# Keys that wait in DRAM with 32 rows per head, and the order of the adds behind a top-1 expert layer

## The chip, the cores and the metric

The kernel runs on one core of one Trainium2 chip, as a single launch. The metric is the time of one execution on the device in microseconds (us). A core has five engines that run side by side, each through its own list of instructions in order: TensorE (PE in the profile, its weight loads PEld), VectorE (DVE), ScalarE (ACT), GpSimd (POOL) and SyncE (SP). They wait for each other by semaphores. SP does not compute; it issues DMA transfers, which 16 DMA engines carry out. ACT and POOL issue some as well.

## The reference, cut to what matters

Eight layers change x, which has 2 batches of 512 tokens with 256 features. Each adds its result, times the tanh of a gate, to x, and starts from a layer norm of x, the last one included. Four of them are attentions to a context of 1024 tokens per batch, and four are feed-forward layers of different kinds.

```python
x = x + tanh(g_xattn[0]) * L0_xattn(ctx, ctx, layernorm(x), ...)   # 5 sampled places per head
x = x + tanh(g_ffn[0])   * L0_ffn(layernorm(x), rhs)               # int8
x = x + tanh(g_xattn[1]) * L1_xattn(layernorm(x), ctx, ctx, ...)   # 16 heads of 8
x = x + tanh(g_ffn[1])   * L1_ffn(layernorm(x), Wg, bg, W1, W2)    # 8 experts, top 1
x = x + tanh(g_xattn[2]) * L2_xattn(layernorm(x), ctx, ctx, ...)   # 16 heads of 16
x = x + tanh(g_ffn[2])   * L2_ffn(layernorm(x), ...)               # ternary weights
x = x + tanh(g_xattn[3]) * L3_xattn(layernorm(x), ctx, ctx, ...)   # 8 heads of 4
x = x + tanh(g_ffn[3])   * L3_ffn(layernorm(x), ...)               # channel mix
```

An attention (l1, l2, l3 below) is, for each head, softmax(scale · Q Kᵀ) V with K and V from the context, and an output product. The expert layer is

```python
gate_scores = softmax(xf @ Wg + bg);  top1 = argmax(gate_scores)
gate = gate_scores * one_hot(top1) / (its sum over tokens + EPS) * T
out  = sum over e of gate[..., e] * (relu(x @ W1[e]) @ W2[e])
```

## The kernel before, in words

x stays in SBUF as 8 blocks of 128 tokens by 256 features: blocks 0 to 3 are batch 0, blocks 4 to 7 batch 1. The context stays there too, transposed.

The kernel is written with a framework that is given tiles (buffers with a tag and a number of copies) and instructions, and that sets semaphores and the order of each engine's instructions by a planner. Where the text calls `keep_in_program_order`, the instruction stays where the program has it. SP keeps at most eight DMAs in flight: each issue first waits for the eighth before it. All its DMAs share one ring on each of the 16 DMA engines, so on one engine they go one after the other; ACT's and POOL's DMAs have rings of their own.

**Keys and values of the attentions.** They depend on the context alone, so they are computed early, in gaps of other layers. During layer 0, `context_1` (L967) computes l1's keys and the values of l1 and l3. TensorE makes `pk` or `pv`, ACT copies it into a staging tile (`kst` L938, `v1st` L983, `v3st` L985, two copies of each tag), and SP stores that to DRAM: K_l1, V_l1, V_l3. In the expert layer `context_2` (L993) computes l2's values, which stay in SBUF, and the keys of l2 and l3, which go to DRAM as K_l2 and K_l3. `prepare_context` (L910) declares these DRAM tensors at the beginning of `context_1`. K has HD + 1 rows of 2048 keys per head (HD is 8, 16 and 4), and the last row, stored from a tile of ones, takes part in the softmax: the query side carries the negated maximum there.

**loaded_keys** (L1013) brings keys to SBUF for groups of four heads. A tile KT has 128 partitions by 2048 keys: head h of the group has partitions 32h to 32h + HD, and the rest of its 32 partitions must be zero, since the score products (L1143, L1174) contract over 32 partitions. So POOL sets the whole tile to zero (L1019), and SP loads each head by a DMA of HD + 1 rows of 8 KB (L1021). l1 and l2 have four groups, l3 has two: 10 memsets and 40 loads. KT tiles have the tag "wide", four buffers that other layers' weights use also.

**Who calls it.** l1's keys and values are loaded at the end of layer 0, when its buffers come free (L1809); the int8 layer runs there. l2's keys are loaded at the end of `moe_ffn` (L1422), each tile when the weights of an expert leave its buffer. l3's are loaded at the end of the ternary layer, from `ternary_ffn` (L1687), before a branch (L1689) that is taken for weights that are not ternary.

**Layer 0** (`window_attention`). For each batch, DVE and ACT make the weights of the sampled places (`window_weights`, L596 to L631, with an exp on ACT at L618). TensorE transposes them (`tpA`), ACT copies that to AT (L440), TensorE spreads AT over the features (L467), and DVE multiplies with the values (`pv` L482, eight per batch).

**The expert layer.** Rows of x are scattered to the experts' places in a DRAM tensor xg, each expert's rows are loaded, go through its two products, and the result `ye` is stored by ACT to the DRAM tensor yg (L1408), two stores per expert. `rest` (L1424) then gathers, per batch, four blocks of rows by an indirect DMA on POOL (L1427) and adds them to x on DVE, times the gate (L1434).

**attention** (L1038) takes `rest` as `before`. It first runs it for batch 0; then batch 0's norm and queries (`queries(0)`) alternate, piece by piece, with `rest` for batch 1. The norm (`statistics` L149, `normalized` L173) is, per batch: statistics of four blocks (L156, L157), variance + eps on DVE (L160), square root on ACT (L161), reciprocal on DVE (L162), the shift nb (L168), h on ACT (L184); TensorE transposes h (L1070) and multiplies by the query weights (L1076).

Of the kernel before, what the change touches and what calls it, by code (L numbers as in the profile page):

```python
# [20 lines left out]
F32 = mybir.dt.float32  # L21
# [4 lines left out]
ALU = mybir.AluOpType  # L26
AX = mybir.AxisListType

P = 128
B, S, D = 2, 512, 256  # L30
M = 1024
# [43 lines left out]
def _bc(ap, shape):  # L75

    return ap.broadcast_to(shape)


class _Net:  # L80
# [829 lines left out]
    def prepare_context(self):  # L910
        nc = self.nc
        self.kd, self.vd = {}, {}
        for name, H, HD in (("l1", 16, 8), ("l2", 16, 16), ("l3", 8, 4)):
            k = self.dram.tile([H, HD + 1, B * M], F32, name=f"K_{name}")
            self.kd[name] = k
            nc.sync.dma_start(
                k[:, HD, :].rearrange("h (c m) -> h c m", m=P),
                _bc(self.ones[:H].unsqueeze(1), [H, B * M // P, P]),
            )
        for name, H in (("l1", 16), ("l3", 8)):  # L920
            self.vd[name] = self.dram.tile([B * M, H * 32], F32, name=f"V_{name}")
# [88 lines left out]

        return V, self.by_key(wv, D, to), keys()

    def loaded_keys(self, name, H, HD):  # L1013

        nc = self.nc
        KT = []
        for g in range(H // 4):
            k = self.wide("KT")([P, B, M])
            nc.gpsimd.memset(k, 0.0)  # L1019
            for h in range(4):  # L1020
                nc.sync.dma_start(  # L1021
                    k[32 * h : 32 * h + HD + 1].rearrange("r b m -> r (b m)"),
                    self.kd[name][4 * g + h],
                )
            KT.append(k)
        return KT

# [10 lines left out]
    def attention(  # L1038
        self, name, KT, V, H, HD, scale, gate, before, bq=None, bv=None, bo=None, aside=None
    ):  # L1040
# [88 lines left out]
        def largest(u, ring=False):  # L1129
# [11 lines left out]
            for i in range(2):  # L1141
                r = 32 * (2 * pair + i)
                nc.tensor.matmul(  # L1143
                    sc[i], lhsT=QT[r : r + 32, g, (b * BPB + k) * P : (b * BPB + k + 1) * P],
                    rhs=KT[g][r : r + 32, b, ts(half, 512)], start=True, stop=True,
                )
# [153 lines left out]
    def moe_ffn(self, gate):  # L1300
        nc, d = self.nc, self.d
# [16 lines left out]
        for n2 in range(NB // 2):  # L1318
            tp = self.ps1.tile([P, DC, 2, P], F32, tag="one", name="tp")
            for k in range(2):  # L1320
                n = 2 * n2 + k
# [7 lines left out]
        p, dest, some, many = self.gates(gate, hT, wg, values)  # L1329
# [68 lines left out]
        def leave(e, h1, w2):  # L1398
            for t in range(2):
                ps = self.ps1.tile([HCAP, D], F32, tag="one", name="py")  # L1400
                for fc in range(HC):
                    nc.tensor.matmul(  # L1402
                        ps, lhsT=h1[:, fc, ts(t, HCAP)], rhs=w2[:, fc, :],
                        start=(fc == 0), stop=(fc == HC - 1),
                    )
                y = self.big.tile([HCAP, D], F32, tag="avj", name="ye", bufs=2)
                self.copy(y, ps)
                nc.scalar.dma_start(self.yg[e * CAP + t * HCAP : e * CAP + (t + 1) * HCAP], y)  # L1408
# [10 lines left out]
            if e + 1 < NE and e + 1 not in ws:  # L1419
                ws[e + 1] = load(e + 1)  # L1420
        leave(*before)
        KT = self.loaded_keys("l2", 16, 16)  # L1422

        def rest(blocks, bank):  # L1424
            y = self.big.tile([P, BPB, D], F32, tag="e", name="yn", bufs=4)
            for k, n in enumerate(blocks):
                nc.gpsimd.indirect_dma_start(  # L1427
                    out=y[:, k, :],
                    out_offset=None,
                    in_=self.yg[:, :],  # L1430
                    in_offset=bass.IndirectOffsetOnAxis(ap=dest[:, n : n + 1], axis=0),
                )
            for k, n in enumerate(blocks):
                nc.vector.scalar_tensor_tensor(  # L1434
                    self.x[:, n, :], y[:, k, :], some[:, n : n + 1], self.x[:, n, :],
                    ALU.mult, ALU.add,
                )
                yield

# [364 lines left out]
    def run(self):  # L1804
        ov = self.out.rearrange("(n p) f -> p n f", p=P)
        self.setup()
        self.sampled_attention()
        self.after_layer_0()
        kv = self.loaded_keys("l1", 16, 8), self.loaded_values("l1", 16)  # L1809
        self.attention(  # L1810
            "l1", *kv, 16, 8, D**-0.5, 1, lambda blocks, bank: self.int8_ffn(4, blocks),
            aside=self.prepare_routing,
        )
        *kv, rest = self.moe_ffn(5)
        self.attention("l2", *kv, 16, 16, 0.25, 2, rest, "bq2", "bv2", "bo2")
        kv, rest = self.ternary_ffn(
            6, lambda: (self.loaded_keys("l3", 8, 4), self.loaded_values("l3", 8))
        )
        scale = float(np.float32(1.0) / np.sqrt(np.float32(32.0)))
        self.attention("l3", *kv, 8, 4, scale, 3, rest, "bq3", "bv3", "bo3")  # L1820
        self.channel_mix_ffn(
            7, lambda n: self.nc.sync.dma_start(ov[:, n, :], self.x[:, n, :])
        )
# [105 lines left out]
```

## Time and profile before

| | us |
|---|---|
| three runs | 1295.62, 1297.02, 1305.35 |
| median | 1297.02 |
| the profiled execution | 1298.23 |
| its span in the profile | 1296.5 |
| TensorE busy | 1156.7 (89%) |
| VectorE busy | 720.3 (56%) |
| ScalarE busy | 607.5 (47%) |
| GpSimd busy | 228.3 (18%) |
| key memsets L1019, ten of 128x2048 | 18.0, mean 1.821 |

The profile is one execution. Its span goes from the first instruction to the last; the profiled execution's own time is 1.7 us longer. The mean granted TensorE clock was 0.933 of full speed. Layers follow each other at about these times: layer 0 until 138, int8 until 165, l1 to about 375, the experts to 562, l2 to about 860, ternary to 1075, l3 to 1244, and the channel mix. A line of a timeline has the start, the duration, the engine, line and operation, output <- inputs, partitions x elements, how many such instructions follow each other, and in brackets how long the engine was idle before and what released it.

### The profile page before, as it was taken

The page shows a single profiled execution, that of the slowest core. Times are in us where ns is not written, and L with a number is a line of the kernel's source. Part 1 is how long each engine was busy: PE and PEld are TensorE (multiplying, and loading weights), DVE is VectorE, ACT ScalarE, POOL GpSimd, SP SyncE. Part 2 cuts the span into 40 slices and gives each one's busy share as a digit, 9 for nine tenths or more (in the row PEclk, how much of TensorE's full clock was granted, in tenths as well). Part 3 has the DMA queues.
Part 4 walks back from the last instruction along what each step waited for, and adds up shares of the span by engine and source line. Part 5 has one row for each costly group of instructions (what it writes and reads, how often), then busy time and mean ns, then how long its engine had stood idle before and what let it go on. Part 6 is the DMA issues. An engine that isn't in the chain of part 4 may idle for free. (4 is left out here: it accounts for less than half of the span.)

```text
span 1296.5 us, 16857 instructions
## 1 busy us (share of the span) xinstructions
PE 1156.7 (89%) x6576; PEld 540.6 (42%) x6596; DVE 720.3 (56%) x1106; ACT 607.5 (47%) x1166; POOL 228.3 (18%) x204
## 2 busy tenths in 40 slices
PE   6987499999998989937999899969999997999977
PEld 3334333333334578823333233334444445543324
DVE  5794678787764111114788778448333111588635
ACT  2422236888874311103488678646333110258761
POOL 1043201334320200131033233000000000113200
PEclk9978698999999989977899999979999998989988
DMA  6033530000211345420000100000122112000000
GB/s 220 1 118 111 116 137 5 1 1 1 66 34 41 111 155 190 156 68 27 16 2 1 66 1 2 17 18 1 34 84 58 58 33 80 9 1 1 10 0 33
DMA packets 56837, 67.49 MB, mean 52 GB/s; under 512 B 4064, under 2 KB 45568, under 8 KB 56288
## 3 DMA queue, kind: packets, MB, share of 16 engines
q1 hardware_dynamic: 52856, 61.07, 15.0%
q0 software_dynamic: 896, 2.49, 0.7%
q10 hardware_dynamic: 2992, 2.70, 0.6%
q8 instruction: 57, 0.93, 0.3%
q14 instruction: 36, 0.29, 0.1%
HBM read 49.93 MB, written 16.32 MB: 51 GB/s over the span
## 5 line engine op out<-in xcount | busy, mean ns | idle before, releaser
L1152 DVE TENSOR_REDUCE part<-scores 128x2 f32<-128x1024 f32 x290 | 341.8, 1219 | 92.5 <-PE bank L1174 77.1
L1179 ACT ACTIVATE e<-bank 128x512 f32<-128x512 f32 x580 | 302.2, 601 | 121.1 <-PE bank L1174 89.4
L1174 PE MATMUL bank<-qa,KT 32*128 32x512 f32 x1160 | 306.1, 634 | 0.6 <-DVE o L1213 0.6
L1143 PE MATMUL scores<-KT,QT 32*128 32x512 f32 x1160 | 293.9, 641 | 4.2 <-DVE part L1152 4.2
L1198 POOL TENSOR_TENSOR avT<-avT,avj 128x512 f32<-128x512 f32 x113 | 143.2, 1268 | 345.9 <-ACT avj L1197 345.9
L1186 PE MATMUL bank<-e,V 128*32 128x512 f32 x1280 | 182.8, 607 | 2.5 <-ACT e L1179 2.5
L1143 PEld LDWEIGHTS scores<-KT,QT 32*128 32x128 f32 x1160 | 100.6, 190 | 157.3 <-DVE part L1152 115.3
L1634 PE MATMUL pg<-hid,wg_h 128*128 128x512 bf16 x752 | 165.1, 379 | 0.8
L1174 PEld LDWEIGHTS bank<-qa,KT 32*128 32x128 f32 x1160 | 117.2, 188 | 36.0 <-issue 18.2
L1634 PEld LDWEIGHTS <-wg_h 128*128 128x128 bf16 x768 | 75.1, 98 | 90.6
L1019 POOL MEMSET KT<- 128x2048 f32 x10 | 18.0, 1821 | 375.9 <-PE pg L1634 157.3
L1186 PEld LDWEIGHTS bank<-e,V 128*32 128x32 f32 x1280 | 28.3, 108 | 106.2 <-ACT e L1179 94.9
L1197 ACT COPY avj<-bank 128x512 f32<-128x512 f32 x113 | 69.2, 612 | 6.7 <-PE bank L1186 6.7
L1402 PE MATMUL py<-w2e,h 128*96 128x256 f32 x256 | 57.4, 379 | 0.0
L1596 DVE TENSOR_REDUCE low<-wg_h 128x1 f32<-128x1024 uint16 x16 | 19.5, 1217 | 57.1 <-DMA wg_h<-in_h2T 54.4
L1606 DVE TENSOR_TENSOR rest<-g,hid 128x512 f32<-128x512 f32 x32 | 21.2, 690 | 51.5 <-ACT hid L1605 51.3
L1070 PE MATMUL bank<-ident,h 128*128 128x128 f32 x48 | 11.7, 369 | 39.0 <-ACT h L184 32.2
L1402 PEld LDWEIGHTS py<-w2e,h 128*96 128x96 f32 x256 | 41.2, 163 | 12.2
L1386 PE MATMUL ph<-xeT,w1e 128*128 128x192 f32 x256 | 45.1, 337 | 0.0
L1386 PEld LDWEIGHTS ph<-xeT,w1e 128*128 128x128 f32 x256 | 43.6, 198 | 1.3 <-DVE xeT L109 0.6
L1076 PE MATMUL bank<-hT,w_l_wq 128*128 128x512 f32 x80 | 41.4, 644 | 2.1 <-DVE part L1150 1.4
L1667 ACT ACTIVATE hid<-pg,cols 128x512 f32<-128x512 f32 x16 | 10.1, 683 | 70.2 <-PE pg L1634 70.2
(303 smaller groups left out, 1325.2 us busy)
## 6 DMA issues: line engine op xcount, KB each, us to landing
w1e<-in_W SPq DMA_DIRECT2D x8, 1024.0 KB
w2e<-in_W SPq DMA_DIRECT2D x8, 1024.0 KB
V_l<-v1st SPq DMA_DIRECT2D x16, 256.0 KB
V<-V_l SPq DMA_DIRECT2D x2, 2048.0 KB
wg_h<-in_h1T SPq DMA_DIRECT2D x8, 512.0 KB
wg_h<-in_h2T SPq DMA_DIRECT2D x8, 512.0 KB
K_l<-kst SPq DMA_DIRECT2D x12, 256.0 KB
KT<-K_l SPq DMA_DIRECT2D x16, 136.0 KB
```

The source lines that it names most:

```text
L1076: nc.tensor.matmul(ps, lhsT=wq[:, dc, ts(c, P)], rhs=hT[:, dc, ts(b, S)], start=(dc == 0), stop=(dc == DC - 1),)
L1143: nc.tensor.matmul(sc[i], lhsT=QT[r : r + 32, g, (b * BPB + k) * P : (b * BPB + k + 1) * P], rhs=KT[g][r : r + 32, b, ts(half, 512)], star ...
L1152: nc.vector.tensor_reduce(to, both, AX.X, ALU.max, negate=True)
L1174: nc.tensor.matmul(t, lhsT=KT[g][r : r + 32, b, ts(j, P)], rhs=augmented[n][r : r + 32, :], start=True, stop=True,)
L1179: nc.scalar.activation(e[:, h, :], t, AF.Exp, scale=scale)
L1186: nc.tensor.matmul(po[32 * h : 32 * h + 32, :], lhsT=V[b][:, j, ts(4 * g + h, 32)], rhs=e[:, h, :], start=True, stop=True,)
L1197: nc.scalar.copy(t, po)
L1198: nc.gpsimd.tensor_tensor(part["oT"], part["oT"], t, ALU.add)
L1386: nc.tensor.matmul(ps[:, k // 2, k % 2, :CAP], lhsT=w1[:, dc, ts(4 * fp + k, P)], rhs=xeT[:, dc, :], start=(dc == 0), stop=(dc == DC - 1),)
L1402: nc.tensor.matmul(ps, lhsT=h1[:, fc, ts(t, HCAP)], rhs=w2[:, fc, :], start=(fc == 0), stop=(fc == HC - 1),)
L1606: nc.vector.tensor_tensor(r, g, hi, ALU.subtract)
L1634: nc.tensor.matmul(ps[:, ts(t, 512)], lhsT=w[:, c, ts(oc, P)], rhs=src(i, c, ts_(t, 512)), start=(c == 0 and i == 0), stop=(c == chunks - ...
```

## The change

K in DRAM gets 32 rows per head. The rows behind the ones are written with zeros, from a new zero tile, by one DMA per attention: 16 × 92 pieces of 2 KB for l1 (3.0 MB), 16 × 60 for l2 (2.0 MB), 8 × 108 for l3 (1.8 MB). They are issued in `prepare_context`, so early in layer 0. `loaded_keys` has no memset any more, and loads a group of four heads as one DMA of 128 rows of 8 KB, 1 MB, where before a head's load had 72 KB in l1, 136 KB in l2 and 40 KB in l3. In `rest` of the expert layer the adds of batch 1 are kept in program order, which has them behind the first pieces of batch 0's norm.

```diff
     def prepare_context(self):
         nc = self.nc
         self.kd, self.vd = {}, {}
+        zero = self.wk.tile([P, 512], F32, tag="wproj", name="zero")
+        nc.gpsimd.memset(zero, 0.0)
         for name, H, HD in (("l1", 16, 8), ("l2", 16, 16), ("l3", 8, 4)):
-            k = self.dram.tile([H, HD + 1, B * M], F32, name=f"K_{name}")
+            k = self.dram.tile([H, 32, B * M], F32, name=f"K_{name}")
             self.kd[name] = k
             nc.sync.dma_start(
                 k[:, HD, :].rearrange("h (c m) -> h c m", m=P),
                 _bc(self.ones[:H].unsqueeze(1), [H, B * M // P, P]),
             )
+            behind = (31 - HD) * B * M // 512
+            nc.sync.dma_start(
+                k[:, HD + 1 :, :].rearrange("h r m -> h (r m)").rearrange("h (c m) -> h c m", m=512),
+                _bc(zero[:H].unsqueeze(1), [H, behind, 512]),
+            )
...
-    def loaded_keys(self, name, H, HD):
+    def loaded_keys(self, name, H):
 
         nc = self.nc
         KT = []
         for g in range(H // 4):
             k = self.wide("KT")([P, B, M])
-            nc.gpsimd.memset(k, 0.0)
-            for h in range(4):
-                nc.sync.dma_start(
-                    k[32 * h : 32 * h + HD + 1].rearrange("r b m -> r (b m)"),
-                    self.kd[name][4 * g + h],
-                )
+            nc.sync.dma_start(
+                k.rearrange("p b m -> p (b m)"),
+                self.kd[name][4 * g : 4 * g + 4].rearrange("h r m -> (h r) m"),
+            )
             KT.append(k)
         return KT
...
+            stay = self.tc.keep_in_program_order if blocks.start else lambda i: i
             for k, n in enumerate(blocks):
-                nc.vector.scalar_tensor_tensor(
-                    self.x[:, n, :], y[:, k, :], some[:, n : n + 1], self.x[:, n, :],
-                    ALU.mult, ALU.add,
+                stay(
+                    nc.vector.scalar_tensor_tensor(
+                        self.x[:, n, :], y[:, k, :], some[:, n : n + 1], self.x[:, n, :],
+                        ALU.mult, ALU.add,
+                    )
                 )
                 yield
```

The calls of `loaded_keys` lose the argument HD. The planner orders some other instructions differently with it. On DVE, the sampling weights of batch 1 in layer 0 (L621 to L631) come ahead of all eight products L482 of batch 0, where four of the products stood among them. On ACT, exp L618 of batch 1 comes ahead of the third and fourth `kst` copy and of AT (L440). On SP, l1's four key loads go ahead of both value loads, where before the first value load went ahead of the sixteen key loads and the second behind them. On DVE at the start of l2, the four adds of batch 1 follow L168 of batch 0's norm.

More of the change, by code (lines that the diff above doesn't have):

```diff
@@ L1421, in moe_ffn @@
         leave(*before)
-        KT = self.loaded_keys("l2", 16, 16)
+        KT = self.loaded_keys("l2", 16)
         def rest(blocks, bank):
@@ L1808, in run @@
         self.after_layer_0()
-        kv = self.loaded_keys("l1", 16, 8), self.loaded_values("l1", 16)
+        kv = self.loaded_keys("l1", 16), self.loaded_values("l1", 16)
         self.attention(
@@ L1816, in run @@
         kv, rest = self.ternary_ffn(
-            6, lambda: (self.loaded_keys("l3", 8, 4), self.loaded_values("l3", 8))
+            6, lambda: (self.loaded_keys("l3", 8), self.loaded_values("l3", 8))
         )
```

## The prediction

> **What bounds the kernel now.** I read the page's first part, then the table of waits, and from there the timelines of the four places that the diff touches.
>
> ```profile
> PE 1156.7 (89%) x6576; PEld 540.6 (42%) x6596; DVE 720.3 (56%) x1106; ACT 607.5 (47%) x1166; POOL 228.3 (18%) x204
> ```
>
> TensorE (PE) is busy 89% of the span and POOL 18%, so an instruction that leaves POOL is worth nothing by itself. The whole group of ten key memsets (18.0 us, 1821 ns each) can bring time only where TensorE idles behind it. TensorE idles in few places; the longest is the start of the second attention (l2), after the experts:
>
> ```profile
> 562.02 0.42 DVE L109 COPY ye<-py 96x256 f32<-96x256 f32 x1 [6.49 <-PE py L1402]
> 562.05 1.80 POOL L1019 MEMSET KT<- 128x2048 f32 x1 [5.10 <-PE py L1402]
> 562.48 0.31 ACTq L1408 DMA_DIRECT2D yg<-ye  x1
> ...
> 563.05 28.29 SPq L1021 DMA_DIRECT2D KT<-K_l  x7
> 569.92 1.05 POOL L1427 DMA_INDIRECT yn<-yg,gt  x1 [6.07 <-DMA KT<-K_l]
> ...
> 579.63 0.48 DVE L1434 SCALAR_TENSOR_TENSOR x<-yn,gt,x 128x256 f32<-128x256 f32 x1 [0.82 <-DMA yn<-yg,gt]
> ...
> ...
> 582.32 0.16 DVE L160 TENSOR_SCALAR rs<-mv 128x4 f32<-128x4 f32 x1
> ...
> 583.53 0.48 DVE L1434 SCALAR_TENSOR_TENSOR x<-yn,gt,x 128x256 f32<-128x256 f32 x1 [1.05 <-DMA yn<-yg,gt]
> 584.81 0.48 DVE L1434 SCALAR_TENSOR_TENSOR x<-yn,gt,x 128x256 f32<-128x256 f32 x1 [0.79 <-DMA yn<-yg,gt]
> ...
> 586.26 0.16 DVE L162 RECIPROCAL rs<-rs 128x4 f32<-128x4 f32 x1
> ...
> 586.65 1.09 ACT L184 ACTIVATE h<-x,nb,rs 128x256 f32<-128x256 f32 x2 [3.93 <-DVE nb L168]
> ...
> 587.31 0.96 PE L1070 MATMUL bank<-ident,h 128*128 128x128 f32 x3 [25.32 <-ACT h L184]
> ```
>
> TensorE waits 25.32 us for h. Before h stand, in a row: the last store of an expert's rows (562.48), the gather that waits for it (569.92, the first of eight, 1.26 us apart), the landing of batch 0's fourth gather, its add on VectorE (DVE) at 579.63, and the norm. The norm's reciprocal L162, ready at about 582.7, stands in DVE's order behind the four adds of batch 1 (581.23, 581.92, and the two shown that wait for their gathers), until 586.26. The norm at the start of l3, where nothing stands between, is the measure:
>
> ```profile
> 1101.32 0.48 DVE L217 SCALAR_TENSOR_TENSOR x<-tw,tg,x 128x256 f32<-128x256 f32 x1
> ...
> 1103.17 0.16 DVE L168 SCALAR_TENSOR_TENSOR nb<-mv,rs 128x4 f32<-128x4 f32 x1
> ```
>
> The start of l1, where four memsets run:
>
> ```profile
> 138.95 7.21 POOL L1019 MEMSET KT<- 128x2048 f32 x4 [14.01 <-PE pso L260]
> ...
> 142.77 3.53 DVE L900 TENSOR_SCALAR qt<-h,lr 128x256 f32<-128x256 f32 x2
> ...
> 146.56 0.39 PE L879 MATMUL tpq<-identb,hq 128*128 128x128 bf16 x2 [7.80 <-DVE hq L901]
> 146.62 0.60 DVE L900 TENSOR_SCALAR qt<-h,lr 128x256 f32<-128x256 f32 x2
> ```
>
> The same two instructions take 3.53 us beside the memsets and 0.60 us just after them, and TensorE waits for their result.
>
> Two stretches show how fast stores and loads can go (columns: start:end, length, busy us and count of PE, PEld, DVE, ACT, POOL, then granted clock, DMA share, GB/s):
>
> ```profile
> 18.00:22.00 4.00, 4.00 (x12) 1.64 (x10) 2.71 (x13) 1.38 (x2) 0.00 (x0) 1.00 1.05 297
> ...
> 180.00:186.00 6.00, 5.63 (x20) 1.98 (x22) 4.65 (x7) 0.82 (x2) 0.00 (x0) 1.00 1.08 386
> ```
>
> **The change part by part.** The sum is made against the profiled execution, 1298.23 us (span 1296.5); it is 1.2 above the median of the runs, 1297.02.
>
> 1. *l1's memsets go.* Two TENSOR_SCALARs fall from 3.53 to 0.60: −2.9. The bounds are 0, if the adds of the int8 stage absorb it, and −2.9; I take −2.9, for TensorE waits right behind. The loads there change from 16 of 72 KB to 4 of 1 MB, and they now go ahead of both value loads (2 MB each) instead of between them: 5.2 MB become 8.2 MB. At 297 to 386 GB/s that is 21 to 28 us from 139: all landed by 160 to 167. First scores need group 0 alone, first in the queue, at 171.7 − 2.9; the values are read from 200. Hidden: even at the slower rate only the last value load lands near the first scores, and its reader comes 30 us later; a stall would start at half that rate.
>
> 2. *Batch 1's adds go behind batch 0's norm.* In l2, from the add at 579.63 to h at 586.65 is 7.02; in l3 the same steps take from 1101.32 to h at 1103.37, 2.05. Difference −5.0, bounds −4.4 (statistics of another block in between) and −5.0. Four adds of 0.48 wait behind L168 instead; who needs them is batch 1's norm, whose h TensorE reaches only after batch 0's transposes and projections, so they are covered; without that cover 4 × 0.48 = 1.9 come back.
>
> 3. *l2's keys.* Before, 16 loads of 17 rows hold SP from 544.48 for 56.49 us: the DMA share in 544 to 556 is 0.10 at 35 GB/s, and in the packet records one engine carries all of it. The last store's and the gathers' share on that engine queues there: the packets of the store at 562.48 end at about 564 on fifteen engines and at 568.26 on that one. After, three of the four loads (1 MB each) run under the experts' products, and the fourth follows the last product at about 562; at 386 GB/s it takes 2.8 us, so behind a start near 563.6 it ends at about 566.4. The store then lands some 1.8 earlier, and the first gather with it: −1.8, bounds 0 (the fourth load in its way costs as much as the slow engine did) and −2.5. The gathers land 5.8 us after issue, by the page's DMA list, and the scatter of rows, of the same kind without such a neighbour, 3.6: bounds 0 and −2.2, I take −1.4, as the two differ in direction. Together −3.2. The keys themselves weren't late before: group 1 lands at 586 and is first read at 626.
>
> 4. *l3's keys.* The memset of 1070.15 and eight loads of 40 KB go; two loads of 1 MB come, the second at about 1070.2. TensorE is at its products until 1075.1 and then waits 8.71 us for its own sequencer at the branch L1689, whose instruction fetch runs beside the value loads (259 GB/s in 1076 to 1084). 1 MB more ahead of those loads, 4 us earlier than the first of them: bounds −1.2 and +1.5; I take −0.5, since the small loads that stood before the values, and the memset that held them, go.
>
> 5. *Layer 0.* New are a 128x512 memset on POOL (0.49, after two of 0.98 for 128x1024) and three stores of zeros on SP, 3.0, 2.0 and 1.8 MB, from partitions 0–15 and 0–7, between the stores of ones and the load of woT, at about 19 us. Their pieces have 2 KB. If they go at the rates above, by engine: engines 0–7 carry 532 KB each, at 386/16 = 24 GB/s 22 us, so until about 42; K_l's first store leaves at 66.66 and between 30 and 60 the DMA moves 0 to 2 GB/s. woT (next in the queue) is read only at 130. Hidden by 20 us. The order of DVE also changes: batch 1's sampling weights (L621 to L631) come ahead of all eight products L482 of batch 0, and ACT takes exp L618 ahead of two key copies. The eight products then run 86.3 to 97 instead of 81.65 to 98.14: −1.0, bounds −1.5 and +2.
>
> Sum: −2.9 − 5.0 − 3.2 − 0.5 − 1.0 = −12.6. **Predicted 1285.6 us** as the profiled execution counts.
>
> [...] The key loads of 9 partitions ran at 87 GB/s in 152 to 158 with a DMA share of 0.58, far under 386, so few partitions can be slow. [...] This trace differs for reads: in the packet records the ones, read from the same 16 partitions in 512-byte pieces, took 27 ns a piece on every engine, and 444 such pieces went by from 19.5 to 20.5, 227 GB/s. No store here reads 16 partitions for longer than 2 us.
>
> **The rivals.**
>
> *Slow zeros (slower than before).* The zeros run at the rate of the 9-partition loads: 6.8 MB at 87 GB/s take 78 us, from 20 to 98. K_l's stores queue behind them on the same rings; ACT copies a third key tile only when the first is stored, and in its new order AT (L440, at 78.89 before) comes after that copy. Decisive point: zeros that end after about 82, under 6.8 MB / 62 us = 110 GB/s, for until then ACT waits for exp at 80.2 anyway. Ending at 98, the copies, the sums on TensorE and AT follow until 101.5, and batch 0's products start at 103, 17 us later than the 86.3 of part 5: 1285.6 + 17 = 1302.6, over the 1298.23 of before. For it speak the 9-partition rows, against it the ones.
>
> *The gathers gain nothing.* The fourth load of keys now uses all 16 engines just as the store is issued. If the store waits out that megabyte, or a gather's landing stays at 5.8, part 3 falls to 0, 1288.8; if the int8 stage also absorbs part 1, 1291.7. For it: the two are issued within 0.5 us. Against: the load is 2.8 us long, the slow engine's backlog reached 568.
>
> *The l3 branch.* The fetch for L1689 falls behind 1 MB more: 4 us at 259 GB/s, 1289.6. Against: the load leaves 4 us before the values.
>
> **How the numbers follow.** Chances: forecast as summed 0.55; gathers without gain, or the branch late, 0.25; slow zeros 0.15; another loss in layer 0 or a throttled clock 0.05. The likeliest case alone spans 1281 (each term at its better bound: −2.9, −5.0, −4.7, −1.2, −1.5 make 1282.9, less about two for the runs' scatter) to 1290. With the rivals the range is 1281 to 1304. A measurement of this kernel tells about 1% from no change: the bounds are 1284.05 and 1309.99. The likeliest case is cut by the lower one: of its 0.55 about 0.33 lies under (the runs' median is 1.2 under the profiled time); of the others almost nothing. Slower by over 1% needs zeros that end after 105 (under 80 GB/s) or the throttled clock: 0.10. That leaves 0.57 for the same.
>
> **What would show it.** Part 1: the first two L900 at 0.6 us, TensorE's wait there near 5. Part 2: from the fourth add to h about 2.1. Part 3: the first gather 5 to 6 us after the last store's issue, not 7.4; 3.6 to 4.6 to landing; TensorE's wait at L1070 near 17. Part 4: the wait at L1689 no longer than 8.7. Part 5: a full DMA share from 19 to about 42 and none from 45 to 66; the pieces of 2 KB near 84 ns. A DMA share of 0.3 to 0.6 that lasts beyond 66, or an AT copy after 90, means slow zeros and makes the forecast wrong.

## The result, and the profile after

The changed kernel takes 1313.76 us (median of five runs, 1312.34 to 1322.30) against 1297.02 before: ratio 1.0128, 95% interval 1.0087 to 1.0168. That is 16.7 us slower, where 1285.6 was forecast with a range up to 1304.

The profiled execution of the changed kernel is the slowest of the five, 1322.3 us at a mean granted TensorE clock of 0.921, so only stretches of it are compared, not its end. From one mark on TensorE to the next, before against after:

| stretch | before | after | difference |
|---|---|---|---|
| start to the output product of layer 0 (pso) | 129.92 | 158.90 | +29.0 |
| pso to the first int8 transpose (tpq) | 16.64 | 13.64 | −3.0 |
| TensorE's wait for h at the start of l2 | 25.32 | 16.35 | −9.0 |
| its wait for the branch at the start of l3 | 8.71 | 8.75 | 0.0 |
| sum | | | +17.0 |

The sum fits the medians' +16.7. The other 7 us of this one execution lie between these marks, 2.7 ahead of l2 and 4.6 behind its start; from 600 to 700 the granted clock is 0.89 in it, and 0.95 in the profile before.

The mark of the first row on TensorE, in the kernel before:

```profile
129.92 8.83 PE L260 MATMUL pso<-w_woT,ctx 128*128 128x256 f32 x32 [3.79 <-PEq L254]
```

and in the changed one:

```profile
158.90 8.75 PE L260 MATMUL pso<-w_woT,ctx 128*128 128x256 f32 x32 [3.68 <-PEq L254]
```

**Layer 0.** The stretches of the changed kernel (columns as in the prediction: granted clock, DMA share and GB/s at the end):

```profile
30.00:40.00 10.00, 10.00 (x32) 2.60 (x30) 9.75 (x19) 4.99 (x8) 0.00 (x0) 0.88 0.91 103
...
50.00:60.00 10.00, 10.00 (x33) 2.37 (x35) 8.14 (x15) 4.06 (x8) 0.00 (x0) 1.00 0.92 103
...
70.00:80.00 10.00, 2.72 (x17) 2.24 (x15) 9.83 (x18) 0.00 (x0) 2.86 (x2) 0.67 0.50 64
...
90.00:100.00 10.00, 0.00 (x0) 0.00 (x0) 0.00 (x0) 0.00 (x0) 0.00 (x0) 0.50 0.51 71
```

The sixteen DMA engines are about 92% busy and move 103 GB/s, where the forecast had 386; a piece of 2 KB takes 293 ns in the packet records, where it took 84 in other stores. From about 68 the share is 0.5: what is left are the zeros of l3, which eight engines carry, from eight partitions, at 52 GB/s in the packet records of 72 to 76, where nothing else moves; the GB/s of the later rows hold other transfers also. In 90 to 100 no engine of the core computes. ScalarE, first in the kernel before, then in the changed one:

```profile
71.01 1.20 ACT L938 COPY kst<-pk 128x512 f32<-128x512 f32 x2 [3.89 <-DMA K_l<-kst]
...
78.89 0.59 ACT L440 COPY AT<-tpA 128x512 f32<-128x512 f32 x1 [6.42 <-PE tpA L437]
```

```profile
66.75 1.05 ACT L945 COPY kst<-pk 128x512 f32<-128x512 f32 x2
80.85 0.47 ACT L618 ACTIVATE sc<-sc 128x320 f32<-128x320 f32 x1 [13.05 <-DVE sc L616]
...
106.49 1.23 ACT L945 COPY kst<-pk 128x512 f32<-128x512 f32 x2 [24.92 <-DMA K_l<-kst]
...
109.45 0.59 ACT L440 COPY AT<-tpA 128x512 f32<-128x512 f32 x1 [1.48 <-PE tpA L437]
```

The third key copy waits 24.92 us for the store of the first (3.89 before), and AT comes behind it, at 109.45 instead of 78.89. From AT to the mark pso the changed kernel takes 49.5 us and the kernel before 51.0, so the loss lies ahead of AT. SyncE, which issues the stores, is held too: its issue of woT lasts 28.26 us (0.58 before), and the first K_l store leaves 9 us later than before. Why that issue lasts so long was not tried.

```profile
47.39 28.26 SPq L120 DMA_DIRECT2D w_woT<-in_woT  x1
75.75 10.04 SPq L951 DMA_DIRECT2D K_l<-kst  x2
```

**The starts of l1 and l2.** In l1 the two TENSOR_SCALARs are short now, and TensorE waits 4.89 instead of 7.80:

```profile
171.67 0.62 DVE L900 TENSOR_SCALAR qt<-h,lr 128x256 f32<-128x256 f32 x2
...
172.54 0.39 PE L879 MATMUL tpq<-identb,hq 128*128 128x128 bf16 x2 [4.89 <-DVE hq L901]
```

In l2 the first gather starts 5.8 us after the last store is issued (7.4 before), the fourth add comes 6.7 after that gather (9.7 before), and h follows that add by 2.7 us (7.0 before):

```profile
591.11 0.31 ACTq L1413 DMA_DIRECT2D yg<-ye  x1
...
596.93 1.04 POOL L1432 DMA_INDIRECT yn<-yg,gt  x1 [118.53 <-issue]
...
603.61 0.48 DVE L1442 SCALAR_TENSOR_TENSOR x<-yn,gt,x 128x256 f32<-128x256 f32 x1 [0.77 <-DMA yn<-yg,gt]
...
606.32 1.09 ACT L184 ACTIVATE h<-x,nb,rs 128x256 f32<-128x256 f32 x2 [0.44 <-issue]
...
606.97 1.18 PE L1075 MATMUL bank<-ident,h 128*128 128x128 f32 x4 [16.35 <-ACT h L184]
```

### The profile page after: what moved, and what is told of

The parts are those of the page before. It is cut to its first block, busy times and chain, and to the rows that moved or that the text cites. A ratio compares the mean times of both kernels' runs of the same rounds, so it can differ in the third digit from the quotient of the medians.

```text
span 1320.6 us, 16784 instructions
## 1 busy us (share of the span) xinstructions
PE 1162.7 (88%) x6576; PEld 543.5 (41%) x6596; DVE 717.3 (54%) x1106; ACT 607.8 (46%) x1166; POOL 209.7 (16%) x195
## 5 line engine op out<-in xcount | busy, mean ns | idle before, releaser
L960 PE MATMUL pv<-w_wv,ctxT 128*128 128x160 f32 (+1 forms) x128 | 32.4, 403 | 33.0 <-ACT kst L945 24.1
L1605 DVE TENSOR_REDUCE low<-wg_h 128x1 f32<-128x1024 uint16 x16 | 19.5, 1217 | 57.4 <-DMA wg_h<-in_h2T 54.4
L960 PEld LDWEIGHTS pv<-w_wv,ctxT 128*128 128x128 f32 x128 | 26.5, 233 | 40.3 <-ACT kst L945 24.5
```

Of the source, the lines that this page charges most:

```text
L960: self.nc.tensor.matmul(ps, lhsT=self.ctxT[:, dc, b, ts(j, P)], rhs=w[:, dc, :], start=(dc == 0), stop=(dc == DC - 1),)
```

## The experiments

The kernel before ran beside each experiment on the same chip, with a median of 1296.8 (e1 to e4), 1297.0 (e5 to e8), 1298.1 (e9, a single run) and 1296.1 (e10). Ratios are to it, with 95% intervals.

**Theory:** the zeros are slow because of the partitions that they are read from, and this holds K_l's stores, ScalarE and AT. **Rivals:** the loss comes from the new order of ScalarE and VectorE, or from the layout with 32 rows; or the rate goes by the number of partitions, not by which ones they are.

### e1: zeros from 128 partitions

```diff
-                k[...].rearrange("h (c m) -> h c m", m=512),
-                _bc(zero[:H].unsqueeze(1), [H, behind, 512]),
+                k[...].rearrange("h (e c m) -> h e c m", e=P // H, m=H * 16),
+                _bc(zero[:, : H * 16].unsqueeze(1), [P, 31 - HD, H * 16]),
```

> The changed kernel, with the zeros read from all 128 partitions of the zero tile (pieces of 1 KB and 512 bytes) where it reads them from partitions 0-15 and 0-7. Theory A (the stores of zeros are slow because of where they are read, and K_l's stores stand behind them on the same rings): zeros done by about 45 us, no 25 us wait of ACT for K_l<-kst, AT copied near 85 instead of 109, so about 29 us less than the changed kernel's 1313.8: 1283 to 1288. Theory B (the loss in layer 0 comes from the new order on ACT and DVE, or from the DRAM layout with 32 rows): no faster than 1308.

Measured: 1287.84 us, ratio 0.9919 (0.9891 to 0.9946). Stretches and ScalarE of e1:

```profile
22.00:30.00 8.00, 7.43 (x37) 5.30 (x38) 5.18 (x11) 1.44 (x5) 0.00 (x0) 0.69 0.95 247
```

```profile
71.60 1.20 ACT L946 COPY kst<-pk 128x512 f32<-128x512 f32 x2 [4.19 <-DMA K_l<-kst]
...
79.19 0.59 ACT L440 COPY AT<-tpA 128x512 f32<-128x512 f32 x1 [6.13 <-PE tpA L437]
```

The rate is 247 GB/s, the zeros end before the first K_l store, AT is copied at 79.19, and 25.9 of the changed kernel's 1313.76 are gone. The layout with 32 rows, the loads of 1 MB and the adds are all still there, so they do not cost the loss. The planner put ScalarE's copies back in the order of before here, so e1 alone does not clear the order; e2 does. e1 is also faster than the kernel before.

### e2: as many partitions, but every fourth

```diff
-                _bc(zero[:H].unsqueeze(1), [H, behind, 512]),
+                _bc(zero[: 4 * H : 4].unsqueeze(1), [H, behind, 512]),
```

> The changed kernel, with the same number of source partitions (16, 16, 8) but every fourth one (0, 4, 8 ... 60). [...] Theory A2 (the rate goes by the number of partitions): 103 GB/s and the piece of 2 KB at 293 ns as in the changed kernel, 1310 to 1316.

Measured: 1291.15 us, ratio 0.9953 (0.9938 to 0.9969). A stretch and ScalarE of e2:

```profile
30.00:40.00 10.00, 9.48 (x30) 1.91 (x28) 9.72 (x18) 4.89 (x8) 0.00 (x0) 1.00 0.93 203
```

```profile
80.56 1.09 ACT L945 COPY kst<-pk 128x512 f32<-128x512 f32 x2
...
84.11 0.59 ACT L440 COPY AT<-tpA 128x512 f32<-128x512 f32 x1 [2.21 <-PE tpA L437]
```

The same number of partitions, the same pieces of 2 KB, the same destinations, and twice the rate: 203 against 103 GB/s, 153 ns a piece against 293. The count of partitions is not what counts. Why partitions four apart go twice as fast as neighbours, no run shows.

e2 keeps the changed kernel's order on ScalarE and VectorE (exp ahead of the third key copy), with zeros that end by 53, and the third key copy waits for no store. AT comes at 84.11 and pso at 133.43, 3.5 later than before. So the order costs about 3, a small part of 29, and it would explain why the time lies over e1's. (The median is 3.3 higher, but the two intervals overlap; the trace is the better measure.) The part of the loss that lies in the rate is therefore about 25.5, from 133.43 in e2 to 158.90 in the changed kernel.

### e3: four staging buffers for keys

```diff
-        staged = lambda tag: lp.tile([P, 512], F32, tag=tag, name=tag, bufs=2)
+        staged = lambda tag: lp.tile([P, 512], F32, tag=tag, name=tag, bufs=4)
```

> The changed kernel with four buffers instead of two for the staged keys in context_1; the zeros stay slow. Theory A with the wait where I put it (ACT's third key copy waits for a store that is behind the zeros, and AT stands behind it in order): no wait at the key copies, AT copied at 82 to 88; the stall moves to the third copy of staged values, which have two buffers, so part of the 29 us comes back, 5 to 20 us: 1294 to 1309. If the products themselves were slowed by the DMA traffic, no change from 1313.8.

Measured: 1303.03 us, ratio 1.0046 (1.0022 to 1.0069). ScalarE of e3:

```profile
78.03 0.58 ACT L440 COPY AT<-tpA 128x512 f32<-128x512 f32 x1 [8.87 <-PE tpA L437]
...
109.05 0.27 ACT L990 COPY v1st<-pv 128x128 f32<-128x128 f32 x1 [15.12 <-DMA V_l<-v1st]
```

The zeros are as slow as in the changed kernel (103 GB/s), yet AT is back at 78.03: the wait at the key copies was the one that held it. The planner also put the key copies and AT ahead of exp again, but that order is worth only about 5 of the 31 us that AT gains (84.11 in e2 against 79.19 in e1). The stall moves to the next tile with two buffers, the staged values, and 10.7 us come back.

### e4: only the adds

The kernel before, with the third part of the diff alone (batch 1's adds kept in program order).

> The kernel before, with only the adds of batch 1 kept in program order behind batch 0's norm. My theory (part 2 of the prediction): from batch 0's fourth add to h 2.1 to 2.8 us instead of 7.02, and 1297.0 - 4.5 = about 1292.5. Rival (the gathers of batch 1 or the one slow DMA engine take the place of the wait): 1296 to 1298.

Measured: 1292.06 us, ratio 0.9970 (0.9948 to 0.9992). TensorE at the start of l2 in e4, which waited 25.32 before:

```profile
584.30 1.18 PE L1070 MATMUL bank<-ident,h 128*128 128x128 f32 x4 [21.34 <-ACT h L184]
```

The wait is 4.0 shorter, the time 4.7.

### e5: the zeros alone

The kernel before, with its own layout, memsets and loads, and the three stores of zeros added into DRAM that nothing reads.

> The kernel before, with the three stores of zeros added, into DRAM that nothing reads; memsets, the 40 key loads and the adds are as before. Theory A (the slow stores alone cost the layer-0 loss): zeros until about 100 to 106, ACT waits for K_l<-kst some 25 us, and the time is 1296.8 + 26 to 30, so 1322 to 1327. Rival (the loss needs the new layout of K_l or the new order): under 1310.

Measured: 1327.02 us, ratio 1.0241 (1.0209 to 1.0274): 30.0 us slower. The table of waits of e5 has the one that was not there before:

```profile
ACT kst L946 <- DMA K_l<-kst: 26.3, 1, 26.3
```

Neither layout nor loads are needed for the loss: the stores make it, with the order on ScalarE that the planner chose here too (exp at 79.22, ahead of the third key copy at 106.21). That this order alone does not make it is shown by e2.

### e6: e1 without the order of the adds

```diff
-            stay = self.tc.keep_in_program_order if blocks.start else lambda i: i
+            stay = lambda i: i
```

> The kernel with zeros from 128 partitions (1287.8), without the program order for batch 1's adds. It leaves the part of the l2 gain that the key loads bring. My split: TensorE's idle before h^T goes from 16.4 to about 20.5 us, the time to about 1292. Rival (the adds no longer matter once the gathers land sooner): idle 16.4, 1288.

Measured: 1290.22 us, ratio 0.9943 (0.9926 to 0.9959). TensorE at the start of l2 in e6:

```profile
581.59 1.18 PE L1076 MATMUL bank<-ident,h 128*128 128x128 f32 x4 [20.45 <-ACT h L184]
```

25.32 becomes 20.45 by the key loads alone (−4.9), 21.34 by the adds alone (e4, −4.0), and 16.35 by both: the two parts add up. Of the time, 2.4 us go back against e1, less than the wait's 4.0 (16.42 in e1); the two ratios' intervals overlap, so the wait is the better measure.

### e7: e1 with l1's memsets

```diff
             k = self.wide("KT")([P, B, M])
+            if name == "l1":
+                nc.gpsimd.memset(k, 0.0)
```

> The kernel with zeros from 128 partitions (1287.8), with l1's four memsets of KT put back ahead of the loads. Part 1 of the prediction: the two TENSOR_SCALAR at 3.5 us again instead of 0.62, TensorE's wait for hq 7.8 instead of 4.9, and 2.9 us more in all, 1290.7. Rival (the later adds absorb it, or the held-back loads cost more): 1288, or over 1293.

Measured: 1288.50 us, ratio 0.9944 (0.9918 to 0.9969), against 0.9919 (0.9891 to 0.9946) for e1. The times do not tell 2.9 us from none. The trace does. VectorE and TensorE of e7:

```profile
146.69 1.92 DVE L871 TENSOR_SCALAR la<-la 128x4 f32<-128x4 f32 x1
...
148.85 1.90 DVE L900 TENSOR_SCALAR qt<-h,lr 128x256 f32<-128x256 f32 x2
...
151.00 0.39 PE L879 MATMUL tpq<-identb,hq 128*128 128x128 bf16 x2 [7.92 <-DVE hq L901]
```

The wait is 7.92 again. The 3 us are split here between a TENSOR_SCALAR of four elements per partition (1.92 instead of 0.17) and the pair (1.90 instead of 0.62), so it isn't one instruction that is slow: the long entries are those beside a memset. The third of the four memsets runs from 146.77 to 148.58 and the fourth from 148.52 to 150.35, which are about the times of the two long entries. Not every instruction beside a memset is longer: the RECIPROCAL between the two takes 0.18 us, as without memsets.

### e8: zeros issued by GpSimd

```diff
-            nc.sync.dma_start(
+            nc.gpsimd.dma_start(
                 k[:, HD + 1 :, :]...
```

> The changed kernel, with the slow stores of zeros issued by POOL instead of SP, so on other rings of the same 16 DMA engines; still from partitions 0-15 and 0-7. If K_l's stores stood behind the zeros because they share rings: the zeros stay slow, but K_l<-kst lands within a few us, ACT's wait at the key copies is under 8 us, time 1284 to 1295. If the engines themselves are held by the slow reads: wait 15 to 25 us, 1303 to 1316.

Measured: 1328.00 us, ratio 1.0226 (1.0205 to 1.0248), worse than both expectations. Now layer 0's inputs come late: TensorE waits 22.76 us for the key weights (w_wk). SyncE and ScalarE in the timeline of e8:

```profile
57.98 27.01 SPq L918 DMA_DIRECT2D K_l<-ones  x3
```

```profile
97.65 0.42 ACT L356 ACTIVATE VW<-edge,cols 128x10 f32<-128x10 f32 x2 [26.03 <-PE edge L351]
```

The zeros begin ahead of the loads of context and weights, and SyncE, which issued the ones at 14.76 before, reaches them at 57.98. Key copies come after the zeros' end here, so this run doesn't tell whether another ring frees K_l's stores. Its packet records do show two rings side by side: from 20 to 50 the zeros, in pieces of 4 KB here (about 600 ns each), move 100 GB/s, and SyncE's loads 37 GB/s, with about as many pieces (674 beside 733). So the loads were not shut out; they got through at about one piece for each slow piece.

### e9: a long store of ones

The kernel before, with one more store: 2.9 MB of ones into DRAM that nothing reads, in 512-byte pieces from partitions 0–15.

> The kernel before, with one more store of ones behind the three, 2.9 MB in the same 512-byte pieces from partitions 0-15, into DRAM that nothing reads: a long case of the pieces that took 27 ns in the profile of before. [...] Rival (small pieces are read at the full rate): 27 ns all through, over 200 GB/s.

Measured: 1300.38 us beside 1298.11, one run each, which gives no verdict on the time. A stretch of e9:

```profile
30.00:40.00 10.00, 9.48 (x29) 1.91 (x28) 9.38 (x17) 4.88 (x8) 0.00 (x0) 1.00 0.77 94
```

In the packet records, of the first 960 pieces of 512 bytes (256 of them a weight's load, 640 the three short stores) nearly all take 27 ns, until 20.5. From about 21.5 on most take 62 to 73, and the rate is 94 GB/s. The ones are about as slow as the zeros once the store is long. So the 27 ns that spoke against slow zeros were a short burst's. Why the first 350 KB go faster was not tried. Shortness alone does not make a store fast: in the changed kernel the ones of l2, 128 KB that stand between the slow zeros, take 55 to 89 ns a piece.

### e10: K_l's and V_l's stores issued by ScalarE

```diff
-                nc.sync.dma_start(self.kd[name][heads, :HD, at : at + 512], k[:n])
+                eng = nc.scalar if name == "l1" else nc.sync
+                eng.dma_start(self.kd[name][heads, :HD, at : at + 512], k[:n])
...
-            nc.sync.dma_start(self.vd["l1"][at], v1[k])
-            nc.sync.dma_start(self.vd["l3"][at], v3[k])
+            nc.scalar.dma_start(self.vd["l1"][at], v1[k])
+            nc.scalar.dma_start(self.vd["l3"][at], v3[k])
```

> The changed kernel with its slow zeros on SP, but the stores of K_l1, V_l1 and V_l3 in layer 0 issued by ACT, so on ACT's rings of the same 16 DMA engines. If the stores stood behind the zeros only because rings are first in, first out: the zeros still run to about 106, but ACT's wait at the key copies is under 6 us, AT is copied before 95, and the time is 1286 to 1297. If the slow reads hold the engines whatever the ring: ACT's wait stays at 15 to 25 us, 1303 to 1316.

Measured: 1335.64 us, ratio 1.0300 (1.0259 to 1.0341). The planner left only l1's zeros early (done by 49), and issued l2's at 97 and l3's at 139.91, so the key copies met no zeros and the values' did. ScalarE's own timeline in e10, and TensorE's:

```profile
99.28 5.00 ACTq L996 DMA_DIRECT2D V_l<-v3st  x1
...
120.12 0.27 ACT L991 COPY v1st<-pv 128x128 f32<-128x128 f32 x1 [5.07 <-DMA V_l<-v1st]
```

```profile
181.73 8.99 PE L260 MATMUL pso<-w_woT,ctx 128*128 128x256 f32 x32 [35.00 <-SPq L254]
```

In the packet records, ScalarE's rings move not one data piece from 97 to 114, though a store was issued on them at 98.92 (the next issue on ScalarE lasted 5.00 us), while SyncE's move l2's zeros at 293 ns a piece. Neither expectation is met as written, since the zeros moved. But a store on other rings of the same engines stood behind the slow reads here, for 15 us. The first rival's "queue behind them on the same rings" is too narrow. l2's zeros are 60 pieces per engine, 60 × 293 ns = 17.6 us, so the hold is nearly as long as that whole store (an estimate from the pieces in the packet records). Why the rings did not take turns here, as they did in e8, where GpSimd issued the zeros, was not tried.

The time of e10 is no measure of that hold. Most of what it loses against the changed kernel is the 35.00 us at the end of layer 0, where TensorE waits at a branch (L254) for SyncE; SyncE had issued l3's zeros at 139.91 and woT at 161.39.

## Why the prediction was wrong

1. *l1's memsets, −2.9: right.* −3.0 in the trace, and e7 brings the wait back. The loads (4 MiB of keys and 4 MiB of values, so 8.4 MB where the text has 8.2) stayed hidden: no wait of TensorE for them stands in the changed kernel's table of waits for l1.
2. *Adds behind the norm, −5.0: right in kind, a little too much.* −4.0 of wait in e4, just outside the bounds of −4.4 to −5.0: h follows the fourth add by 2.71 us there, where the norm of l3 had 2.05.
3. *l2's keys, −3.2: right in kind, too little.* −4.9 in e6. The part between the store and the gather was −1.6 (taken −1.8); the landing, from the first gather to the fourth add, −3.0 (taken −1.4, with a bound of −2.2).
4. *l3's keys, −0.5: nothing.* 8.71 against 8.75, inside the −1.2 to +1.5 that was given.
5. *Layer 0, −1.0: this step failed, +29.0.* The step was "If they go at the rates above, by engine: engines 0–7 carry 532 KB each, at 386/16 = 24 GB/s 22 us, so until about 42". The 386 GB/s is the rate of stores from 128 partitions (xg and yg); the zeros have 16 and 8. They moved 103 GB/s, then 52 on half of the engines, and ended at 106. The sign that the prediction had named for this came: a DMA share of 0.5 beyond 66, and AT after 90. What spoke against it, the 9-partition loads at 87 GB/s, was named, and set aside for "444 such pieces went by from 19.5 to 20.5, 227 GB/s". e9 shows that this row measured a burst of 350 KB; the text had seen itself that no store read 16 partitions for longer than 2 us, and still let that decide over 6.8 MB. The 9-partition loads, nearer in duration, were near the 79 GB/s that the zeros made on average (6.8 MB in 86 us). The order's −1.0 failed too, by less: e2 has it as +3.5. There the products of batch 0 start at 86.55, as forecast, but they end at 102.9 and not at 97, since after the fourth they wait 4.68 and 1.23 us for TensorE's pw, which the forecast left out.

The first rival had the mechanism: slow zeros, ScalarE's wait at the third key copy, AT behind it. Its price, 17, was too small. It had one rate for all zeros, 87 GB/s until 98; the run had 103 for l1 and l2 and half of the engines for l3, so 106: 8 us more. And it was set against a layer 0 that the new order speeds up by 1; e2 shows that this order costs about 3. With both, 17 + 8 + 4 is the 29 that was measured. The wait at exp until 80.85, from which it took the point where the zeros begin to cost, was in place. It had a chance of 0.15, though one of the two measurements at hand, the 9-partition rows, spoke for it.

Without part 5 the sum is −2.9 − 5.0 − 3.2 − 0.5 = −11.6 against the run's −3.0 − 9.0 = −12.0. That the two agree is in part luck, as part 2 was too large and part 3 too small. e1, which mends part 5 alone, is 9.0 faster than before by the medians; in its profile layer 0 is 1.1 longer than before, the other two stretches 3.0 and 8.9 shorter.

## What to carry to other kernels

A store that is meant to be hidden is costed by where its source lies, not by its bytes alone: spread the source over more partitions, as e1 does (all 128) for one changed access pattern and 26 us; in e2 no more partitions than in the changed kernel, but four apart (203 GB/s against 103), brought most of it. A burst of a few hundred KB is no measure for a store of MBs; look for a row of the same duration, or make one, as e9 does. And when a slow DMA goes early, ask which later transfers share its engines and which engine waits for them in order: here two staging buffers tied ScalarE, then TensorE, to the end of the zeros.

## What the runs showed of the hardware that was not expected

- Which partitions, not how many: 16 neighbours 103 GB/s, 16 that lie four apart 203, 128 partitions 247 (in smaller pieces; why no more was not tried).
- The first 350 KB or so of narrow stores went at 27 ns per 512 bytes, the rest mostly at 62 to 73 (e9).
- SyncE itself is held behind slow stores: an issue that took 0.58 us before lasted 28.26.
- ScalarE's rings moved no data piece for 15 us after a store was issued on them, while SyncE's rings on the same engines moved slow zeros (e10). With the zeros on GpSimd's rings, SyncE's loads got through at about one piece for each slow piece (e8).
